# Deformed convolution: GpSimd adds two columns of a neighbourhood to two others in 8 of 20 units, in written order; TensorE turns a unit one unit later

## The chip, the cores and the metric

The kernel runs on one core of a Trainium2 chip. A core has five engines, each with its own queue of instructions that it works off in order: TensorE (PE: matrix products, and with the identity as one operand also transposes; its weight loads are shown apart as PEld), VectorE (DVE), ScalarE (ACT), GpSimd (POOL) and SyncE (SP, which here only issues DMAs). Engines wait for each other through semaphores. Data lies in SBUF (128 partitions), and TensorE writes its results to PSUM, which ScalarE and VectorE read. The metric is the device time of one execution in microseconds (us), as the median of several runs. A profiled execution gives a trace of every instruction.

## The reference, cut to what matters

The whole computation is a small network of four layers on an image of 256 channels and 64 x 64 points. The change concerns layer 1, a deformable convolution (3 x 3 points, 8 groups of 32 channels):

```python
v = x_nhwc @ w_in + b_in
f = gelu(layer_norm(depthwise_conv_3x3(x)))
offset = (f @ w_off + b_off).reshape(B, H, W, G, P, 2)
mask = softmax((f @ w_mask + b_mask).reshape(B, H, W, G, P), axis=-1)
# each of the 9 points of a group is read bilinearly at its shifted place
sampled = gather(y0, x0) * (1 - wx) * (1 - wy) + gather(y0, x1) * wx * (1 - wy) \
        + gather(y1, x0) * (1 - wx) * wy       + gather(y1, x1) * wx * wy
out = (sampled * mask).sum(points) @ w_out + b_out
y = batch_norm(out);  return y * sigmoid(y)
```

The offsets are small (under one point), so the kernel does not gather: each output point is a weighted sum over the 5 x 5 neighbourhood of `v`, with 25 weights for each point and group that it works out from offsets and mask. The input is checked for that at the end, and another path, not run here, is there for larger offsets.

## The kernel before, in words

`layer1_near` runs over 8 blocks (`b`), each of 4 image rows in the upper half and 4 in the lower half: partitions are 64 columns of the upper half and 64 of the lower. A block is worked in 20 **units** `(r, dy)`: row `r` (0 to 3) of the block times row `dy` (0 to 4) of the neighbourhood, in the order r, then dy. In what follows a unit has its number 5r + dy, 0 to 19.

For a unit, one multiplication forms the five products of the neighbourhood's columns `dx` with their weights, as a tile `pr` of 128 x 1280 (5 columns x 256 channels). Then TensorE transposes each of the five columns in two halves of 128 channels, and all these transposes accumulate in one PSUM tile `acc`: the transposes are at once the turn from points to channels and the sum over the 25 neighbours. A unit has 10 transposes of 128 x 128; I call them the unit's **turn** (L1152 to L1156). For dy = 0 to 3 VectorE makes the product (L1150), into one of three buffers (`bufs=3`), with weights that ScalarE has copied to PSUM (`l_w_ps`, L1132, one buffer for two rows r). For dy = 4 GpSimd makes it (L1145, `pr4`, one buffer), and it is issued when the row's unit dy = 0 is written.

After units 9 and 19 ScalarE copies `acc` (L1160), two output projections follow (`project`, L1163 to L1169: TensorE, then Silu on ScalarE, then an add on VectorE), and at the end of a block the results are turned back to tokens (`tokens`, L1171). These go through a list, `late`, from which one entry is taken after each unit.

Beside the units of block b, work for later blocks is woven in, by the number of the unit at which it is written:

- `near_offsets(b + 2)`: the depthwise convolution as 18 taps, two each at units 0 to 8 (ScalarE scales a shifted image, L1011 and L1013, into one of three buffers, and TensorE turns and accumulates it with 4 transposes, L1015); the layer norm at unit 9 on VectorE (statistics L1022, scaling `l_n` L1029); turns and Gelu at 15 and 16 (L1036, L1038); the projection to offsets and mask at 18 and 19 (L1043, one PSUM buffer, read by VectorE in L1044). Blocks 0 to 5 have this.
- `near_weights(b + 1)`: from these offsets and masks the 25 weights, mostly on GpSimd: the softmax's subtraction (`powers`, unit 0, L1068) and division (`shares`, unit 2, L1083), `across` (unit 4, L1086), `columns` 0, 1 and 2 (units 6, 8 and 10, L1094 and L1097: 3, 4 and 4 instructions), `rows` (units 11 to 15, L1105 to L1109). VectorE and ScalarE give it maxima, sums, exponentials and hat functions. Blocks 0 to 6 have this.

Within `manual_schedule` (L953) TensorE's instructions keep the order in which they are written. The order on the other engines is decided by a scheduler. On GpSimd it has put all of a block's `near_weights` between the `pr4` of row 0 and that of row 1.

Of the kernel before, what the change touches and what calls it, by code (L numbers as in the profile page):

```python
# [10 lines left out]
F32 = mybir.dt.float32  # L11
# [3 lines left out]
ALU = mybir.AluOpType  # L15
# [4 lines left out]
P = 128  # L20
# [60 lines left out]
def bc(ap, axis, n):  # L81

    ap = ap.unsqueeze(axis)
    shape = list(ap.shape)
    shape[axis] = n
    return ap.to_broadcast(shape)


class Net:
# [28 lines left out]
    def weights(self, pool, names):  # L118

        for i, name in enumerate(names):  # L120
            src = self.A[name].rearrange("(k p) n -> p k n", p=P)
            w = pool.tile(list(src.shape), F32, tag=name, name=name)
            eng = self.nc.sync if i % 2 == 0 else self.nc.scalar
            eng.dma_start(out=w, in_=src)
            self.w[name] = w
# [785 lines left out]
    def layer1_near(self, y, t, xd, pool, dpool, wp, ps):  # L911
        nc, w = self.nc, self.w
        bn_s, bn_t = self.bn(pool)


        vt = dpool.tile([VW, VW, C], F32, tag="vt", name="vt")
        zero = pool.tile([P, 2 * C], F32, tag="zero", name="zero")
        nc.gpsimd.memset(zero, 0.0)
        for at in (0, VW - 2):
            edge = vt[at : at + 2].rearrange("a b c -> (a b c)").rearrange("(p k) -> p k", p=P)  # L920
            nc.scalar.dma_start(out=edge, in_=zero[:, : edge.shape[1]])
            nc.scalar.dma_start(out=vt[2 : HW + 2, at : at + 2, :].rearrange("a b c -> a (b c)"), in_=zero[:HW, :])
        def values(b):
            vs = wp.tile([P, TPB, C], F32, tag="vs", name="l1_v", bufs=2)
            for i in range(0, TPB, 2):
                p = ps.tile([P, 2, C], F32, tag="acc", name="l1_v_ps", bufs=2)
                for j in range(2):
                    r = b * TPB + i + j
                    for kt in range(2):
                        for h in range(2):  # L930
                            nc.tensor.matmul(p[h * HW : (h + 1) * HW, j, :], y[:, kt, h, r + 1, 1 : HW + 1],
                                             w["w_in1"][:, kt, :], start=(kt == 0), stop=(kt == 1))
                nc.vector.tensor_add(vs[:, i : i + 2, :], p, bc(self.row("b_in"), 1, 2))
            for h in range(2):
                r0 = HH * h + b * TPB + 2
                nc.sync.dma_start(out=vt[2 : HW + 2, r0 : r0 + TPB, :], in_=vs[h * HW : (h + 1) * HW])

        vks = []
        def chunk(k):

            vk = pool.tile([P, 5, 2, C], F32, tag="vk", name="l1_vk", bufs=4)
            for h in range(2):
                for dx in range(5):
                    r0 = HH * h + 2 * k
                    nc.sync.dma_start(out=vk[h * HW : (h + 1) * HW, dx], in_=vt[dx : dx + HW, r0 : r0 + 2, :])
            vks.append(vk)

        spare = pool.tile([P, NBLK], F32, tag="spare", name="l1_spare")


        offsets = lambda b: self.near_offsets(b, y, wp, ps)
        weights = lambda b, om: self.near_weights(b, om, spare, wp)
        with self.tc.manual_schedule(engines={mybir.EngineType.PE}):  # L953
            om, wg = {}, {}
            om[0], todo = offsets(0)
            for b in range(NBLK):
                values(b)
                for _, go in todo[3 * b : 3 * b + 3]:
                    go()
            for k in range(3):  # L960
                chunk(k)
            for _, go in todo[3 * NBLK :]:
                go()
            wg[0], todo = weights(0, om[0])
            om[1], more = offsets(1)
            for _, go in todo + more:
                go()
            late = []
            for b in range(NBLK):
                beside = []  # L970
                if b + 1 < NBLK:
                    wg[b + 1], todo = weights(b + 1, om[b + 1])
                    beside += todo
                if b + 2 < NBLK:
                    om[b + 2], todo = offsets(b + 2)
                    beside += todo
                units, end = self.near_products(b, xd, t, wg[b], vks, chunk, bn_s, bn_t, wp, ps)
                for u, unit in enumerate(units):
                    late += unit()
                    for at, go in beside:  # L980
                        if at == u:
                            go()
                    if late:
                        (late.pop(0) or (lambda: 0))()
                late += end
            for go in late:
                go and go()

        low = pool.tile([P, 1], F32, tag="low", name="l1_low")
        nc.vector.tensor_reduce(low, spare, AX.X, ALU.min)  # L990
        nc.vector.tensor_single_scalar(self.flags[:, 0:1], low, 0.0, ALU.is_lt)
# [123 lines left out]
    def near_products(self, b, xd, t, wg, vks, chunk, bn_s, bn_t, wp, ps):  # L1115
# [3 lines left out]
        nc, w = self.nc, self.w  # L1119
        R = TPB  # L1120
# [3 lines left out]
        def start(i):  # L1124
            if i == 0:
                for m in range(2):
                    nc.scalar.dma_start(out=sx[:, m], in_=xd[m].rearrange("p (h r x) -> p h r x", h=2, x=HW)[:, :, b * R : (b + 1) * R])
                    nc.scalar.activation(sx[:, m], sx[:, m], AF.Identity, bias=self.par("bout0", m))
            if 2 * b + i + 3 < 2 * NBLK + 2:
                chunk(2 * b + i + 3)  # L1130
            held["w"] = ps.tile([P, 2, 5, 5, NH], F32, tag="w", name="l1_w_ps")
            nc.scalar.copy(held["w"].rearrange("p r a b g -> p (r a b g)"), wg[:, 2 * i : 2 * i + 2].rearrange("p r a b g -> p (r a b g)"))  # L1132
            held["acc"] = ps.tile([P, 2, 2, P], F32, tag="acc", name="l1_acc_ps", bufs=2)

        def unit(r, dy):
            i, j = r // 2, r % 2
            if j == 0 and dy == 0:
                start(i)
            acc, at = held["acc"], r + dy
            vk = vks[2 * b + at // 2][:, :, at % 2, :].rearrange("p d (g c) -> p d g c", c=D)  # L1140
            if dy == 0:

                vk4 = vks[2 * b + (r + 4) // 2][:, :, r % 2, :].rearrange("p d (g c) -> p d g c", c=D)
                held["pr4"] = wp.tile([P, 5, NH, D], F32, tag="pr4", name="l1_pr4", bufs=1)
                nc.gpsimd.tensor_tensor(held["pr4"], vk4, bc(wg[:, r, 4], 3, D), ALU.mult)  # L1145
            if dy == 4:
                pr = held["pr4"]
            else:
                pr = wp.tile([P, 5, NH, D], F32, tag="pr", name="l1_pr", bufs=3)
                nc.vector.tensor_tensor(pr, vk, bc(held["w"][:, j, dy], 3, D), ALU.mult)  # L1150
            pf = pr.rearrange("p d g c -> p d (g c)")
            for dx in range(5):  # L1152
                for m in range(2):
                    nc.tensor.matmul(acc[:, m, j, :], pf[:, dx, m * P : (m + 1) * P], self.ident, is_transpose=True,  # L1154
                                     start=(j == 0 and dy == 0 and dx == 0 and m == 0),
                                     stop=(j == 1 and dy == 4 and dx == 4 and m == 1))  # L1156
            if j == 0 or dy < 4:
                return []
            aT = wp.tile([P, 2, 2 * P], F32, tag="aT", name="l1_aT")
            nc.scalar.copy(aT, acc.rearrange("p m j q -> p m (j q)"))  # L1160
            return [None] + [(lambda m: lambda: project(i, aT, m))(m) for m in range(2)]

        def project(i, aT, m):  # L1163
            o = ps.tile([P, 2, 2, HW], F32, tag="o", name="l1_o_ps")
            self.mm(o.rearrange("p j h x -> p (j h x)"), [(w["w_out1"][:, kt, m * P : (m + 1) * P], aT[:, kt, :]) for kt in range(2)])
            sl = wp.tile([P, 2, 2, HW], F32, tag="sl", name="sl")
            nc.scalar.activation(sl, o, AF.Silu, bias=bn_t[:, m : m + 1], scale=bn_s[:, m : m + 1])
            xs = sx[:, m, :, 2 * i : 2 * i + 2].rearrange("p h r x -> p r h x")
            nc.vector.tensor_add(xs, xs, sl)  # L1169
# [1744 lines left out]
```

## Time and profile before

| what | value |
|---|---|
| median of 3 runs | 3446.09 us (3445.12 to 3449.45) |
| profiled execution, its own time | 3443.01 us |
| its span in the profile | 3441.5 us |
| TensorE busy in the span | 3103.2 us (90%) |
| VectorE busy | 2311.1 us (67%) |
| GpSimd busy | 1457.5 us (42%) |
| stretch of layer 1's units | 1097 to 1433 us of the span |
| transposes of units (L1154) in it | 1600 |

The page gives busy times over the whole span, and most of the span is other layers. What matters here are the 336 us from 1097 to 1433 us, in which the eight blocks are worked; so the stretch's own tables are read: busy time by engine, what an instruction waited for, and the timeline. Two things help in reading them. A merged row of the timeline gives when a group started and how long it lasted, with the modelled end of the last matrix product in it. And idle time of an engine is printed with what ended it.

### The profile page before, as it was taken

The page shows a single profiled execution, that of the slowest core. Times are in us where ns is not written, and L with a number is a line of the kernel's source. Part 1 is how long each engine was busy: PE and PEld are TensorE (multiplying, and loading weights), DVE is VectorE, ACT ScalarE, POOL GpSimd, SP SyncE. Part 2 cuts the span into 40 slices and gives each one's busy share as a digit, 9 for nine tenths or more (in the row PEclk, how much of TensorE's full clock was granted, in tenths as well). Part 3 has the DMA queues.
Part 4 walks back from the last instruction along what each step waited for, and adds up shares of the span by engine and source line. Part 5 has one row for each costly group of instructions (what it writes and reads, how often), then busy time and mean ns, then how long its engine had stood idle before and what let it go on. Part 6 is the DMA issues. An engine that isn't in the chain of part 4 may idle for free.

```text
span 3441.5 us, 66218 instructions
## 1 busy us (share of the span) xinstructions
PE 3103.2 (90%) x25772; PEld 2319.7 (67%) x25772; DVE 2311.1 (67%) x5339; ACT 1327.2 (39%) x2554; POOL 1457.5 (42%) x1323
## 2 busy tenths in 40 slices
PE   6779999999977899896969789999999996999997
PEld 3443444344436888665857567888888885999996
DVE  8885777577754677796855576777777775555552
ACT  4444334444425666242633352222222222333331
POOL 2028788778843555326344352000000003555552
PEclk9889999999988999897979899999999997999998
DMA  2146556521134222100158643323333214555554
GB/s 74 40 114 142 161 154 168 130 68 52 48 116 111 68 74 73 44 1 2 52 183 264 215 181 127 98 86 98 99 99 98 91 64 154 200 194 199 206 206 176
DMA packets 241688, 407.01 MB, mean 118 GB/s; under 512 B 78353, under 2 KB 152850, under 8 KB 231890
## 3 DMA queue, kind: packets, MB, share of 16 engines
q1 hardware_dynamic: 212002, 344.40, 32.2%
q0 software_dynamic: 13056, 35.93, 2.8%
q10 hardware_dynamic: 16304, 22.31, 1.9%
q8 instruction: 207, 3.39, 0.4%
q14 instruction: 119, 0.97, 0.1%
HBM read 287.07 MB, written 111.30 MB: 116 GB/s over the span
## 4 chain that ended last, share of the span: by engine, by line
PE 42%; DVE 9%; DMA 5%; issue 5%; ACT 3%; POOL 3%; SPq 0%; POOLq 0%; DVEq 0%; ACTq 0%
PE a_sa_ps L2537 6%; PE f_h_ps L146 5%; DMA ys<-f_y,f_at 3%; PE l_acc_ps L1154 3%; PE a_oa_ps L2576 3%; PE a_ob_ps L2576 3%; PE a_oc_ps L2576 3%; PE a_sb_ps L2537 3%; PE f_ya_ps L146 2%; PE f_yb_ps L146 2%; POOL ys L2292 2%; DVE l_pr L1150 2%; PE a_od_ps L2576 1%; PE a_q_ps L146 1%; PE a_qkv_ps L146 1%
## 5 line engine op out<-in xcount | busy, mean ns | idle before, releaser
L770 ACT COPY l_sc<-l_s 128x384 f32<-128x384 f32 (+1 forms) x632 | 304.0, 532 | 456.9 <-PE l_s L763 445.0
L775 DVE TENSOR_TENSOR l_sm<-l_s,mask 128x256 f32<-128x256 f32 (+2 forms) x628 | 308.2, 552 | 89.2 <-PE l_s L763 88.0
L2103 POOL DMA_INDIRECT xs<-f_room,f_to x64 | 64.5, 1007 | 698.0 <-issue 582.4
L146 PE MATMUL f_h_ps<-f_xT,f_w 128*128 128x256 f32 x1440 | 341.1, 388 | 19.4 <-DVE f_xT L2212 9.7
L146 PEld LDWEIGHTS f_h_ps<-f_xT,f_w 128*128 128x128 f32 x1440 | 262.2, 192 | 84.0 <-ACT f_h L2222 31.3
L763 PE MATMUL l_s<-l_q,l_k 32*128 32x256 f32 (+3 forms) x2944 | 270.5, 453 | 0.0
L2556 ACT ACTIVATE a_e<-a_e 128x512 f32<-128x512 f32 x256 | 156.0, 629 | 246.2 <-DVE a_e L2526 245.2
L780 POOL TENSOR_TENSOR l_sm<-l_sc,mask 128x768 f32<-128x768 f32 (+1 forms) x116 | 201.9, 1748 | 88.2 <-ACT l_sc L770 88.1
L2222 ACT ACTIVATE f_h<-f_h_ps,f_w 128x256 f32<-128x256 f32 x360 | 166.6, 470 | 187.9 <-PE f_h_ps L146 178.7
L1150 DVE TENSOR_TENSOR l_pr<-l_vk,l_w_ps 128x1280 f32<-128x1280 f32 x128 | 186.7, 1482 | 55.2 <-PE l_acc_ps L1154 37.6
L763 PEld LDWEIGHTS l_s<-l_q,l_k 32*128 32x128 f32 x2944 | 132.4, 183 | 115.2 <-issue 67.5
L2292 POOL DMA_INDIRECT ys<-f_y,f_at x144 | 145.7, 1012 | 140.6 <-ACT f_y L2291 110.0
L1154 PE MATMUL l_acc_ps<-ident,l_pr 128*128 128x128 f32 x1600 | 198.1, 278 | 7.7 <-POOL l_pr L1145 7.6
L1154 PEld LDWEIGHTS l_acc_ps<-ident,l_pr 128*128 128x128 f32 x1600 | 184.7, 144 | 14.1 <-POOL l_pr L1145 8.3
L784 POOL TENSOR_TENSOR l_sm<-l_sc,mask 128x256 f32<-128x256 f32 (+1 forms) x220 | 184.9, 868 | 16.1 <-ACT l_sc L770 15.2
L2249 POOL TENSOR_TENSOR f_wt<-f_w 128x512 f32<-128x512 f32 x72 | 89.8, 1268 | 217.1 <-PE f_ya_ps L146 204.9
L2537 PE MATMUL a_sa_ps<-a_q,a_kt 128*128 128x256 f32 x512 | 155.6, 386 | 15.1 <-DVE a_u L2542 14.3
L2541 ACT COPY a_u<-a_sa_ps 128x256 f32<-128x256 f32 x128 | 47.6, 372 | 292.0 <-PE a_sa_ps L2537 292.0
L809 PE MATMUL l_b_ps<-l_sm,l_v 128*32 128x256 f32 (+2 forms) x2176 | 153.7, 372 | 0.0
L2537 PE MATMUL a_sa_ps<-a_qt,a_kt 128*128 128x256 f32 x512 | 152.3, 379 | 0.0
L780 POOL TENSOR_TENSOR l_sm<-l_sc,mask_c 128x768 f32<-128x768 f32 (+1 forms) x64 | 122.9, 1937 | 39.7 <-ACT l_sc L770 39.2
L2537 PE MATMUL a_sb_ps<-a_qt,a_kt 128*128 128x256 f32 x512 | 131.4, 379 | 0.0
(558 smaller groups left out, 7292.1 us busy)
## 6 DMA issues: line engine op xcount, KB each, us to landing
a_kt<-a_kd SPq DMA_DIRECT2D x128, 512.0 KB
f_w<-in_f_w SPq DMA_DIRECT2D x36, 1152.0 KB
f_w<-in_f_w SPq DMA_DIRECT2D x36, 1028.0 KB
xs<-zero SPq DMA_DIRECT2D x8, 4160.0 KB
l_vk<-vt SPq DMA_DIRECT2D x180, 128.0 KB
f_x<-xs SPq DMA_DIRECT2D x72, 260.0 KB
f_w<-in_f_w SPq DMA_DIRECT2D x36, 384.0 KB
l_rcp<-l_recd SPq DMA_DIRECT2D x48, 256.0 KB
```

Source lines behind the costliest of these rows:

```text
L146: self.nc.tensor.matmul(out, lhsT, rhs, start=(i == 0), stop=(i == len(pairs) - 1))
L763: nc.tensor.matmul(s[pair, j][:, at : at + m, :], key(hp), qs[hp], start=(z == 0), stop=(z == len(pieces) - 1))
L770: nc.scalar.copy(sc[:, j], s[1, j])
L775: nc.vector.tensor_tensor(to(pair, j, kind, at), pick(s[pair, j], kind, which), mask, ALU.mult)
L780: nc.gpsimd.tensor_tensor(out[:, :, at, :], of[:, :, which, :], bc(mask, 1, 2), ALU.mult)
L784: nc.gpsimd.tensor_tensor(to(1, j, kind, at), pick(sc[:, j], kind, which), mask, ALU.mult)
L1150: nc.vector.tensor_tensor(pr, vk, bc(held["w"][:, j, dy], 3, D), ALU.mult)
L1154: nc.tensor.matmul(acc[:, m, j, :], pf[:, dx, m * P : (m + 1) * P], self.ident, is_transpose=True, start=(j == 0 and dy == 0 and dx == 0 a ...
L2222: nc.scalar.activation(h[:, m, :], q, AF.Gelu, bias=w1[:, 2 * hidden + m : 2 * hidden + m + 1])
L2292: nc.gpsimd.indirect_dma_start(out=self.ys_parts[(i % 4) * NI + k], in_=y[:, k, :], in_offset=None, out_offset=bass.IndirectOffsetOnAxis(a ...
L2537: mm = lambda out, i, right: nc.tensor.matmul(out, A[i], right, start=True, stop=True)
L2576: nc.tensor.matmul(out, vs[:, j, i, :], right, start=(j == 0 and side != 1), stop=(j == NPAIR - 1 and side != 0))
```

## The change

Four things change in the units.

1. In units with dy = 1 or 3 (8 of 20) GpSimd adds columns 2 and 3 of the product tile to columns 0 and 1, in place (an add of 128 x 512), and TensorE then turns only the columns 0, 1 and 4: 6 transposes instead of 10.
2. The turn of a unit is written one unit later: `unit()` now returns a function, and the loop calls it in the next unit (`behind`), before that unit's woven work. `after` keeps a block's end in place behind it.
3. GpSimd's instructions, too, keep the order in which they are written.
4. In the block's last row (r = 3) VectorE makes the product of dy = 4 too, so GpSimd has three `pr4` in a block and not four.

```diff
-        with self.tc.manual_schedule(engines={mybir.EngineType.PE}):
+        with self.tc.manual_schedule(engines={mybir.EngineType.PE, mybir.EngineType.Pool}):
...
-            late = []
+            late, behind, after = [], lambda: [], []
...
                 for u, unit in enumerate(units):
-                    late += unit()
+                    use = unit()
+                    late += behind() + after
+                    behind, after = use, []
                     for at, go in beside:
                         if at == u:
                             go()
                     if late:
                         (late.pop(0) or (lambda: 0))()
-                late += end
-            for go in late:
+                after = end
+            for go in late + behind() + after:
...
-            if dy == 0:
+            by_pool = r < R - 1
+            if dy == 0 and by_pool:
...
-            if dy == 4:
+            if dy == 4 and by_pool:
                 pr = held["pr4"]
...
-            for dx in range(5):
-                for m in range(2):
-                    nc.tensor.matmul(acc[:, m, j, :], pf[:, dx, m * P : (m + 1) * P], self.ident, is_transpose=True,
+            columns = range(5)
+            if dy in (1, 3):
+                nc.gpsimd.tensor_tensor(pf[:, 0:2], pf[:, 0:2], pf[:, 2:4], ALU.add)
+                columns = (0, 1, 4)
+
+            def use():
+                for dx in columns:
+                    for m in range(2):
+                        nc.tensor.matmul(acc[:, m, j, :], pf[:, dx, m * P : (m + 1) * P], self.ident, is_transpose=True,
...
+            return use
```

More of the change, by code (lines that the diff above doesn't have):

```diff
@@ L1151, in unit @@
             pf = pr.rearrange("p d g c -> p d (g c)")
-            for dx in range(5):
-                for m in range(2):
[L1154 to L1161, printed above, removed]
+            columns = range(5)
[6 more added lines that the diff above has]
+                        nc.tensor.matmul(acc[:, m, j, :], pf[:, dx, m * P : (m + 1) * P], self.ident, is_transpose=True,
+                                         start=(j == 0 and dy == 0 and dx == 0 and m == 0),
+                                         stop=(j == 1 and dy == 4 and dx == 4 and m == 1))
+                if j == 0 or dy < 4:
+                    return []
+                aT = wp.tile([P, 2, 2 * P], F32, tag="aT", name="l1_aT")
+                nc.scalar.copy(aT, acc.rearrange("p m j q -> p m (j q)"))
+                return [None] + [(lambda m: lambda: project(i, aT, m))(m) for m in range(2)]
+            return use
         def project(i, aT, m):
```

## The prediction

> **What bounds the kernel now.** I read the stretch of layer 1's units alone, 1097 to 1433 us. First its busy times, by parts: a steady block, then block 6 up to its unit 11, then the rest (columns: length, busy time of PE, PEld, DVE, ACT, POOL, granted clock, DMA share, GB/s).
>
> ```profile
> core 0: us, PE busy (x) PEld busy (x) DVE busy (x) ACT busy (x) POOL busy (x), PEclk, DMA share, GB/s
> 1231.70:1276.05 44.35, 40.41 (x323) 38.52 (x322) 32.09 (x40) 29.88 (x45) 25.36 (x24) 0.96 0.25 72
> 1364.60:1390.50 25.90, 19.71 (x142) 18.43 (x141) 18.61 (x19) 10.91 (x16) 20.37 (x22) 0.87 0.25 72
> 1390.50:1433.00 42.50, 39.42 (x325) 37.15 (x323) 31.74 (x29) 8.73 (x16) 12.22 (x8) 1.00 0.16 41
> ```
>
> A steady block takes 44.3 us, TensorE is busy 91% of it; VectorE has 12 us to spare, GpSimd 19. Second, who waits for whom in the stretch:
>
> ```profile
> POOL l_pr L1145 <- PE l_acc_ps L1154: 83.3, 16, 6.5
> DVE l_pr L1150 <- PE l_acc_ps L1154: 37.6, 33, 5.2
> PE l_f_ps L1015 <- ACT l_tap L1013: 13.7, 6, 2.5
> PE l_acc_ps L1154 <- POOL l_pr L1145: 7.6, 2, 4.0
> ```
>
> VectorE and GpSimd wait for TensorE to free their buffers; TensorE waits little for products. So it is the bound, with gaps. Third, prices, by form (mean ns of one after the busy time; the last row is from later, the nearest to the new add: in place, 128x512, two inputs):
>
> ```profile
> L1154 PE MATMUL l_acc_ps<-ident,l_pr 128*128 128x128 f32 x1600 | 198.1, 278 | 7.7 <-POOL l_pr L1145 7.6
> L1150 DVE TENSOR_TENSOR l_pr<-l_vk,l_w_ps 128x1280 f32<-128x1280 f32 x125 | 182.3, 1482 | 51.6 <-PE l_acc_ps L1154 37.6 <-ACT l_w_ps L1132 12.6 <-DMA l_vk<-vt 0.2
> L1094 POOL TENSOR_TENSOR l_tx<-l_ax,l_hat 128x288 f32<-128x288 f32 x35 | 28.5, 829 | 0.6
> L1094 POOL TENSOR_TENSOR l_tmp<-l_ax,l_hat 128x288 f32<-128x288 f32 x28 | 21.9, 804 | 0.0
> L1097 POOL TENSOR_TENSOR l_tx<-l_tx,l_tmp 128x576 f32<-128x576 f32 x14 | 19.9, 1418 | 0.6
> L1145 POOL TENSOR_TENSOR l_pr<-l_vk,l_wg 128x1280 f32<-128x1280 f32 x31 | 72.8, 2348 | 95.4 <-PE l_acc_ps L1154 83.3 <-issue 9.0 <-DMA l_vk<-vt 3.1
> L1674 POOL TENSOR_TENSOR t<-t,pr 128x512 f32<-128x512 f32 x16 | 17.5, 1093 | 0.0
> ```
>
> Last, the timeline of a steady block, at the points that I measure from, and one row of block 6:
>
> ```profile
> 1231.57 1.25 PE L1154 MATMUL l_acc_ps<-ident,l_pr 128*128 128x128 f32 x10
> 1245.50 1.25 PE L1154 MATMUL l_acc_ps<-ident,l_pr 128*128 128x128 f32 x10
> 1253.87 2.35 POOL L1145 TENSOR_TENSOR l_pr<-l_vk,l_wg 128x1280 f32<-128x1280 f32 x1
> 1259.46 1.25 PE L1154 MATMUL l_acc_ps<-ident,l_pr 128*128 128x128 f32 x10
> 1260.75 1.49 DVE L1150 TENSOR_TENSOR l_pr<-l_vk,l_w_ps 128x1280 f32<-128x1280 f32 x1
> 1275.88 1.26 PE L1154 MATMUL l_acc_ps<-ident,l_pr 128*128 128x128 f32 x10
> ...
> 1383.73 4.53 PE L1154 MATMUL l_acc_ps<-ident,l_pr 128*128 128x128 f32 x20 [3.54 <-POOL l_pr L1145]
> ```
>
> These are the turns of unit 0 (T0, right after the second offset projection), 4, 11 and the next T0; 1253.87 is row 1's pr4, 1260.75 unit 15's product. Ten turns back to back advance by 1.09 us (pitch 0.109; the modelled end hangs over by 0.16). So a block has three parts: **I**, T0 to the end of turn 4, 15.03; **II**, to the end of turn 11 (1260.55), 13.95; **III**, to the next T0, 15.33. The row at 1383.73 shows what a wait costs afterwards: 20 transposes in 4.53 us, 0.227 each, at a granted clock of 0.50 (1383.7 to 1388.2).
>
> **The change part by part.**
>
> *Fewer transposes:* 8 x 4 in a block, 32 x 0.109 = 3.5 us of TensorE, 28 us in all; a gain where TensorE stays the bound.
>
> *Adds in written order.* The build order of the changed kernel on GpSimd is, after T0: softmax subtraction, add 1, division, add 3, `across`, pr4 of row 1, add 6, `columns` 0, add 8, `columns` 1, pr4 of row 2, `columns` 2, add 11, `rows` with add 13, adds 16, 18, the next pr4. Row 1's pr4 has one buffer and waits for turn 4. Before, it stood behind all weights too, but only unit 9 needed it, at 1256.27; it was done at 1256.22. Now turn 11 needs add 11, and between turn 4 and that lies, on one queue: 2.35 (pr4) + 1.09 + 3 x 0.83 + 1.09 + (2 x 0.80 + 0.83 + 1.42) + 2.35 + (the same 3.85) + 1.09 = 18.2 us, and 0.2 for two semaphores. TensorE has only this to do meanwhile: turns 5 to 10 (52 transposes, 5.7), taps of four units (8 groups of 4, 3.5), two token turns (0.9), a projection (1.0): 11.1 us. It waits 7.3 us, mostly before turn 11, then makes that turn at half clock, 6 x 0.227 = 1.4. Part II becomes 19.8: **+5.8**. Queued behind turn 11 on TensorE is the second output projection and every later turn; VectorE's unit 15 waits for the buffer that turn 11 frees.
>
> The add is not in the trace. Low: 1.05 (the scaling in place of L1671). High: 1.47 (L2249's form with `f_wt` as input and output). I take L1674's 1.09, which is an add in place like this one; 1.47 makes II 1.1 longer.
>
> *One unit later, and the last row's product on VectorE.* Part III is VectorE's: in before, from unit 15's product, through scaling `l_n`, three products, the weight copy, three products, to L1044, which frees the PSUM buffer that the second offset projection waits for (1.47 us of wait there). In the built order it is after `l_n` units 16 to 19, the copy and next unit 0: five products in place of six. **-1.4** (one at 1.43 back to back). TensorE's 22 transposes fewer in III (turns 12 to 18, 58, for 12 to 19, 80) are beside it: no further gain. The bound: 0 if add 16 or 18 holds up TensorE's first projection, -2.9 if the copy's wait (0.6) and the clock are better too.
>
> *Part I* has the same TensorE work (turns 19 to 4 are 52 transposes in place of 50) and the same chain of L1044, maximum, subtraction, exponential, tap, which in before stops TensorE for 2.45 us. But ScalarE's built order now puts the Silu of the first output projection behind the fourth to sixth tap and a table load (1.28), and the second projection waits for it. Worked along the queue this is 0.4 to 1.2 later; I take **+0.8**, ends 0 and 2. Adds 1 and 3 are done 1 us before their turns.
>
> *Sum.* A steady period gets +5.8 - 1.4 + 0.8 = +5.2. There are five from T0 to T0 (1142.9 to 1364.5): +26. Block 0: unit 4 a slot later (+1.0), part II 19.8 instead of 18.8 (1108.47 to 1127.28, TensorE waited 4.0 for pr4 there already), -1.4: +0.6. Block 6, without taps: T0 to the end of turn 11 was 25.95; now `across` ends at +9.3, pr4 starts at +9.7, and with 18.4 and 1.4 it is 29.5: +3.5. Block 6's end and block 7, 35.8 us before: TensorE saves 44 x 0.109 = 4.8, but VectorE makes 22 products instead of 20 (22 x 1.44, eight adds of 0.42, three copies' waits of 0.6: 36.9), and twice a pr4 and an add (3.5) stand against 2 us of TensorE work: +2, ends -3 and +4. Total **+32**, on 3443.0: 3475. That execution is 3.1 us under the median of the runs shown, 3446.1; on the median it is **3478**. SP's queue is the same; outside the stretch nothing moves.
>
> *Two rules against the trace.* The Trainium skill, "TensorE: Matmul & The Clock Gate", Part 4, says that the full clock does not engage for transposes. Here 90 transposes from 1391.28 took 9.99 us at a clock of 1.00, so the rule does not hold; by it the 256 transposes saved would be worth 58 us. The same page's closing table wants no idle gap over about 3 us; the trace is stricter: after 2.45 us idle (1236.09 to 1238.54) the clock was 0.59 until 1242.7. By either, a 7 us wait is followed by slow turns.
>
> **The rivals.**
>
> 1. *TensorE stays the bound* (other side). Its work per block falls by 3.5 us, and nothing waits: -28, **3418**. For it: 91% busy, GpSimd idle 19 us a block, and it would be busy 32 of 41. Against it: it needs GpSimd's 18.4 us to be at most about 13 (the point where the period is 44.3 again), and the prices and the buffer's wait leave no room.
> 2. *It comes out even*, within 7 us: the waits of part I (2.45 and 1.1) vanish and III takes its lower end: +5.0 - 2.9 - 2.0 = 0.1 a period; **3448**. Against it: the exponential's chain is untouched.
> 3. *Worse*: adds of 1.47, half clock also in parts I and III: +5.8 + 1.1 + 2 + 0 = +8.9 a period, five of them 45, with block 0 (2), 6 (5) and the end (4) +56: **3502**. For it: GpSimd's add may price like L2249.
> 4. *It does not do what it says*: excluded, since the built order has 64 adds on GpSimd and 1344 turns' transposes.
>
> **How the numbers follow.** Forecast 0.72, worse 0.15, even 0.06, TensorE-bound 0.07. What can be told from no change is 0.2%, 7 us. Low end of the likeliest: 3.4 a period (no slow clock, part I at 0, adds 1.05), +17, and the tail -3: 3460; I reach to 3453 for part of the even case. High: 3502, the worse case. Slower 0.88, same 0.05, faster 0.07.
>
> **What would show it.** Right: a steady period of about 49.5 us; "PE l_acc_ps <- POOL l_pr" near 5 to 7 us a block, in turn 11, with a clock near 0.5 behind it; GpSimd's pr4 of row 2 back to back with the two `columns`; VectorE's unit 15 right after turn 11. Wrong: a period under 44, or TensorE waits spread over VectorE's products. An add far from 1.09 us, or `columns` slowed beside the adds, would miss the size.

## The result, and the profile after

The changed kernel takes 3483.9 us (median of 4 runs, 3478.2 to 3491.0), the kernel before 3447.4 us beside it (3445.1 to 3449.5). The ratio is 1.0107, with a 95% interval of 1.0087 to 1.0127: slower, by 36.5 us, where 32 were forecast. The profiled execution took 3485.17 us (span 3483.4), 42.2 more than the profiled execution of before.

In the trace, the stretch of layer 1's units begins with the second offset projection ahead of them (1096.32 us before, 1094.17 after) and ends with a DMA that loads the next layer's `w_qkv` (1430.00 and 1470.57). That is 333.7 us before and 376.4 after, 42.7 more: the whole loss lies in the stretch. First, the busy times of the changed kernel (columns as in the table of before): a steady block from T0 to T0, block 6 up to the end of its turn 11, and the rest.

```profile
core 0: us, PE busy (x) PEld busy (x) DVE busy (x) ACT busy (x) POOL busy (x), PEclk, DMA share, GB/s
1244.12:1292.90 48.78, 37.97 (x290) 35.45 (x289) 34.91 (x41) 29.99 (x45) 32.70 (x31) 0.93 0.23 66
...
1391.89:1425.10 33.21, 20.16 (x131) 18.07 (x130) 21.54 (x20) 11.27 (x17) 25.57 (x24) 0.85 0.19 56
1425.10:1470.57 45.47, 37.25 (x277) 33.09 (x275) 35.19 (x28) 7.34 (x14) 22.18 (x18) 0.96 0.10 30
```

This block is 4.4 us longer than the one shown of before (the mean over five is 5.0), and no engine is busy more than 78% of it: TensorE has less work and more time. Second, the waits in the stretch, 1097 to 1471 us (who waits for whom: total us, number, longest):

```profile
PEld l_acc_ps L1163 <- POOL l_pr L1157: 70.7, 27, 7.4
PE l_acc_ps L1163 <- POOL l_pr L1157: 62.5, 21, 7.0
DVE l_pr L1153 <- PE l_acc_ps L1163: 61.7, 32, 6.5
POOL l_pr L1157 <- DVE l_pr L1153: 42.7, 18, 4.1
POOL l_pr L1148 <- PE l_acc_ps L1163: 38.6, 9, 6.0
```

Before, TensorE waited 7.6 us for GpSimd in the whole stretch; now it waits 62.5 us, all of it for the new add (L1157). Third, the prices, by form:

```profile
L1153 DVE TENSOR_TENSOR l_pr<-l_vk,l_w_ps 128x1280 f32<-128x1280 f32 x133 | 194.0, 1481 | 79.1 <-PE l_acc_ps L1163 61.7 <-ACT l_w_ps L1134 10.6 <-DMA l_vk<-vt 5.6
L1163 PE MATMUL l_acc_ps<-ident,l_pr 128*128 128x128 f32 x1344 | 179.7, 287 | 62.9 <-POOL l_pr L1157 62.5 <-DVE l_pr L1153 0.2
L1157 POOL TENSOR_TENSOR l_pr<-l_pr 128x512 f32<-128x512 f32 x64 | 82.0, 1282 | 44.3 <-DVE l_pr L1153 42.7 <-DMA l_vk<-vt 1.6
L1148 POOL TENSOR_TENSOR l_pr<-l_vk,l_wg 128x1280 f32<-128x1280 f32 x23 | 54.1, 2352 | 38.6 <-PE l_acc_ps L1163 38.6
```

The add takes 1.28 us, not the 1.09 that I took. VectorE's product kept its price beside the adds (1.48 us before and after), so the loss is not a slower VectorE. Last, the timeline of the steady block: T0, row 1's `pr4`, `columns` 1's last instruction, row 2's `pr4`, add 11, turn 11, unit 15's product, and the next T0. (In the changed kernel the turn at T0 is that of unit 19, written one unit late.)

```profile
1244.12 1.25 PE L1163 MATMUL l_acc_ps<-ident,l_pr 128*128 128x128 f32 x10
...
1259.26 2.35 POOL L1148 TENSOR_TENSOR l_pr<-l_vk,l_wg 128x1280 f32<-128x1280 f32 x1 [5.27 <-PE l_acc_ps L1163]
...
1268.61 1.42 POOL L1099 TENSOR_TENSOR l_tx<-l_tx,l_tmp 128x576 f32<-128x576 f32 x1
...
1269.99 2.34 POOL L1148 TENSOR_TENSOR l_pr<-l_vk,l_wg 128x1280 f32<-128x1280 f32 x1
...
1276.08 1.26 POOL L1157 TENSOR_TENSOR l_pr<-l_pr 128x512 f32<-128x512 f32 x1
...
1277.39 1.54 PE L1163 MATMUL l_acc_ps<-ident,l_pr 128*128 128x128 f32 x6 [7.03 <-POOL l_pr L1157]
...
1279.04 1.49 DVE L1153 TENSOR_TENSOR l_pr<-l_vk,l_w_ps 128x1280 f32<-128x1280 f32 x1 [5.68 <-PE l_acc_ps L1163]
...
1292.90 1.25 PE L1163 MATMUL l_acc_ps<-ident,l_pr 128*128 128x128 f32 x10
```

GpSimd starts row 1's `pr4` when turn 4 has freed its buffer, and from there it is busy without a gap until add 11: 1259.26 to 1277.34. TensorE has nothing left from 1270.36 on and waits 7.03 us. Turn 11 starts when add 11 ends, and runs slowly: its six transposes take 1.34 us to the start of the next projection at 1278.73, 0.22 each. The windows around it show the granted clock (third column from the right):

```profile
1270.30:1277.39 7.09, 0.06 (x1) 0.00 (x1) 3.06 (x4) 3.33 (x4) 7.09 (x7) 0.84 0.00 0
1277.39:1280.40 3.01, 3.01 (x10) 2.58 (x11) 1.36 (x1) 0.00 (x0) 2.93 (x6) 0.50 0.04 8
```

### The profile page after: what moved, and what is told of

It is laid out like the page before. It is cut to its first block, busy times and chain, and to the rows that moved or that the text cites. A ratio compares the mean times of both kernels' runs of the same rounds, so it can differ in the third digit from the quotient of the medians.

```text
span 3483.4 us, 65789 instructions
## 1 busy us (share of the span) xinstructions
PE 3091.9 (89%) x25516; PEld 2301.6 (66%) x25516; DVE 2345.7 (67%) x5347; ACT 1326.5 (38%) x2554; POOL 1517.0 (44%) x1379
## 4 chain that ended last, share of the span: by engine, by line
PE 64%; DVE 14%; DMA 7%; POOL 5%; issue 5%; ACT 4%; SPq 1%; ACTq 0%; POOLq 0%; DVEq 0%
PE l_s L763 9%; PE a_sa_ps L2548 6%; PE f_h_ps L146 5%; PE l_b_ps L809 4%; DMA ys<-f_y,f_at 3%; PE a_oa_ps L2587 3%; PE a_ob_ps L2587 3%; PE a_oc_ps L2587 3%; PE l_a_ps L809 3%; PE a_sb_ps L2548 3%; PE l_x_ps L146 3%; PE f_ya_ps L146 2%; PE l_c_ps L809 2%; PE f_yb_ps L146 2%; PE l_acc_ps L1163 2%
## 5 line engine op out<-in xcount | busy, mean ns | idle before, releaser
L1153 DVE TENSOR_TENSOR l_pr<-l_vk,l_w_ps 128x1280 f32<-128x1280 f32 x136 | 198.4, 1481 | 83.5 <-PE l_acc_ps L1163 61.7
L1163 PE MATMUL l_acc_ps<-ident,l_pr 128*128 128x128 f32 x1344 | 179.7, 287 | 62.9 <-POOL l_pr L1157 62.5
L1163 PEld LDWEIGHTS l_acc_ps<-ident,l_pr 128*128 128x128 f32 x1344 | 162.1, 149 | 75.7 <-POOL l_pr L1157 70.7
L780 POOL TENSOR_TENSOR l_sm<-l_sc,mask_c 128x768 f32<-128x768 f32 (+1 forms) x64 | 121.0, 1906 | 39.3 <-ACT l_sc L770 38.7
```

The lines of the kernel that those rows point to most:

```text
L780: nc.gpsimd.tensor_tensor(out[:, :, at, :], of[:, :, which, :], bc(mask, 1, 2), ALU.mult)
```

## The experiments

**The theory**: the adds make TensorE late, because they stand on a queue in written order behind a `pr4` that waits for its one buffer and behind two `columns`. **Rivals**: the turn one unit later or the moved product of the last row loses the time; or each add costs its share, wherever it stands. No variant leaves out a part of the computation: where adds are taken away, those units make all ten transposes again. The runs were made on several chips, whose times differ by up to 2%, so only the ratio to the kernel before on the same chip is compared. The period is that of five steady blocks, between the starts of the second offset projections; the "end" is from the last of these to the `w_qkv` load. Both come from one profiled execution of each kernel. Expectations in microseconds stand against 3447 us.

| kernel | ratio (95%) | period, us | end, us |
|---|---|---|---|
| before | 1 | 44.3 | 67.1 |
| before, GpSimd in written order | 0.9983 (0.9973 to 0.9992) | 44.3 | 66.9 |
| after | 1.0107 (1.0087 to 1.0127) | 49.3 | 80.2 |
| no adds | 0.9958 (0.9941 to 0.9974) | 43.4 | 63.7 |
| two buffers for `pr4` | 1.0084 (1.0067 to 1.0101) | 47.9 | 75.7 |
| `columns` 2 one unit later | 1.0076 (1.0059 to 1.0093) | 47.8 | 74.0 |
| GpSimd ordered by the scheduler | 1.0113 (1.0096 to 1.0130) | 48.2 | 82.9 |
| adds 1, 3, 13, 16, 18 | 1.0048 (1.0026 to 1.0069) | 47.1 | 73.3 |
| adds 6, 8, 11 | 1.0134 (1.0118 to 1.0151) | 51.2 | 76.7 |
| adds 1, 3, 6, 8, 16, 18 | 0.9999 (0.9988 to 1.0009) | 44.1 | 72.9 |
| adds 1, 3, 16, 18 | 0.9966 (0.9952 to 0.9980) | 42.5 | 69.7 |
| adds 11, 13 | 1.0100 (1.0083 to 1.0116) | 49.4 | 74.5 |
| adds 11, 13; `columns` 2 behind add 13 | 0.9988 (0.9979 to 0.9998) | 44.7 | 69.6 |
| adds 1, 3, 16, 18 in blocks 0 to 5 | 0.9935 (0.9919 to 0.9952) | 42.6 | 65.2 |

### 1. No adds

```diff
-                nc.gpsimd.tensor_tensor(pf[:, 0:2], pf[:, 0:2], pf[:, 2:4], ALU.add)
-                columns = (0, 1, 4)
+                pass
```

> The changed kernel without GpSimd's adds: every unit is turned with 10 transposes again; written order, later turn and VectorE's product in the last row stay. Theory (the queue on GpSimd from pr4 of row 1 to add 11 holds up turn 11): no turn waits for an add, part II falls from 19.7 to the 13.0 to 13.9 us of TensorE's work, parts I and III stay near 15.5 and 14.2; a steady period near 43.2 us, 1.1 under before's 44.3, block 6 loses its 3.5 us wait too: 3432 to 3442 us. Rival (written order, the later turn or VectorE's extra product cost the time): the period stays above 46 us and the time above 3455 us.

Measured: ratio 0.9958, which is 3433 us on 3447; the period is 43.4 us. The other three parts of the change are a gain of 0.4%, and the adds cost 1.5%, net of the transposes that they save. The rival that the later turn or the moved product loses the time falls.

### 2. Two buffers for `pr4`

```diff
-  held["pr4"] = wp.tile([P, 5, NH, D], F32, tag="pr4", name="l1_pr4", bufs=1)
+  held["pr4"] = wp.tile([P, 5, NH, D], F32, tag="vs", name="l1_pr4", bufs=2)
```

(The other tag is one whose space lies free here.)

> The changed kernel with two buffers for GpSimd's products of dy = 4 (they take over the place of an earlier tile, vs, that is no longer needed). Theory: pr4 of row 1 no longer waits for turn 4 and starts some 5 us earlier, but add 8 then waits for VectorE's product of unit 8, whose buffer turn 5 frees, so only about 2 us of the 7 us wait before turn 11 go: a period near 47.2 us, 3474 us. Rival (the one buffer is the cause): the wait before turn 11 goes to under 2 us, a period of 44.5 us, 3455 us.

Measured: 1.0084, period 47.9 us, near what the theory has; the rival's 44.5 us falls. The buffer is worth 1.4 us of the 5.0. The waits between 1100 and 1430 us and the turn 11 of one block in this kernel:

```profile
POOL l_pr L1157 <- DVE l_pr L1153: 50.4, 23, 4.2
PE l_acc_ps L1163 <- POOL l_pr L1157: 45.5, 15, 7.0
```

```profile
1221.24 1.54 PE L1163 MATMUL l_acc_ps<-ident,l_pr 128*128 128x128 f32 x6 [5.42 <-POOL l_pr L1157]
```

TensorE still waits 5.4 us in turn 11. With `pr4` earlier, GpSimd's adds wait for VectorE's products instead (50.4 us in total; between the same times the changed kernel has 31.3, and 55.9 for TensorE's waits): in a written order an add that comes too early blocks `columns`, which could have run.

### 3. `columns` 2 and the rows one unit later

```diff
-  [(6 + 2 * kx, call(columns, kx)) for kx in range(3)]  ...  [(11 + dy, call(rows, dy)) for dy in range(5)]
+  [((6, 8, 11)[kx], call(columns, kx)) for kx in range(3)]  ...  [(12 + dy, call(rows, dy)) for dy in range(5)]
```

> The changed kernel with the third group of columns written at unit 11 instead of 10, behind add 11, and the rows one unit later (12 to 16). Theory: the queue from turn 4 to add 11 is 3.7 us shorter, the wait before turn 11 falls from 7 to about 3.3 us, a wait of up to 1.8 us before turn 13 appears beside VectorE's work; a period near 45.2 us, 3455 to 3463 us. Rival (the adds cost by their number and price, wherever they stand): GpSimd's work is the same, so the time stays within 5 us of the changed kernel's.

Measured: 1.0076, or 3474 us, period 47.8 us: more than the theory's 3455 to 3463, and 10 us below the changed kernel, where the rival allowed 5. The mechanism was half right. Turn 11 waits 3.26 us, but `columns` 2 are now ahead of add 13, and in some blocks turn 13 waits too. The timeline of one such block:

```profile
1219.55 0.88 PE L1163 MATMUL l_acc_ps<-ident,l_pr 128*128 128x128 f32 x6 [3.26 <-POOL l_pr L1157]
...
1224.98 3.61 PE L1163 MATMUL l_acc_ps<-ident,l_pr 128*128 128x128 f32 x16 [2.59 <-POOL l_pr L1157]
```

The second wait, 2.59 us, is followed by turns 13 and 14 in 3.6 us (16 transposes, 0.226 each). So in this block, and in one more of the five, the time came back one turn later. In the other three turn 11 itself ran slowly behind its wait of 2.6 to 3.3 us, and turn 13 waited 1.2 us or not at all. I had looked only at the turn whose wait I moved.

### 4. GpSimd ordered by the scheduler

```diff
-        with self.tc.manual_schedule(engines={mybir.EngineType.PE, mybir.EngineType.Pool}):
+        with self.tc.manual_schedule(engines={mybir.EngineType.PE}):
```

> The changed kernel with GpSimd's order left to the scheduler, which puts add 3 behind all three groups of columns and pr4 of row 1 behind all of the block's weights. Theory: turn 3 waits for add 3 until about T0 + 20 us instead of being due at 13.4, so part I grows by some 7 us to 22, and part II shrinks to 13.5 since add 6 to add 11 then stand close together: a period near 49.7 us, 3475 to 3490 us, with the wait moved from turn 11 to turn 3. Rival (the written order is what costs): a period near 43 us, under 3447 us.

Measured: 1.0113, within the interval of the changed kernel; period 48.2 us. I had expected the wait in turn 3 and a period of 49.7. The scheduler puts all `columns` and `rows` ahead of add 6, not of add 3, so the wait stands in turn 6 instead of turn 11 (GpSimd's last row and add 6, then turn 6, in this kernel):

```profile
1219.58 0.32 POOL L1107 COPY l_wg<-l_tx 128x160 f32<-128x160 f32 x1
1219.85 1.26 POOL L1157 TENSOR_TENSOR l_pr<-l_pr 128x512 f32<-128x512 f32 x1
```

```profile
1221.17 1.34 PE L1163 MATMUL l_acc_ps<-ident,l_pr 128*128 128x128 f32 x6 [3.59 <-POOL l_pr L1157]
```

So it is not the written order as such. And written order does no harm to the kernel before either:

### 5. The kernel before, with GpSimd in written order

```diff
-        with self.tc.manual_schedule(engines={mybir.EngineType.PE}):
+        with self.tc.manual_schedule(engines={mybir.EngineType.PE, mybir.EngineType.Pool}):
```

> The kernel before with one edit: GpSimd's instructions in written order. Theory: row 1's pr4 no longer stands behind all weights, so the waits for it in block 0 (4.0 us) and block 6 (3.5 us) go; the steady period stays near 44.3 us: ratio 0.997 to 0.998, which would be most of what the changed kernel without adds gains (0.9958). Rival (the later turn or VectorE's product in the last row makes that gain): ratio 0.999 to 1.001.

Measured: 0.9983 (0.9973 to 0.9992), a gain of about 0.2%, with the steady period and the end unchanged. The gain is in block 0, where TensorE waited 4 us for a `pr4` before: from its second offset projection to the next one it takes 39.3 us instead of 45.1. The wait for a `pr4` in block 6, which I expected to count as well, is gone without making the end shorter. Together with the first experiment this gives the parts of the change: written order -0.2%, the later turn and the moved product about another -0.2% (period 43.4 instead of 44.3, end 63.7 instead of 66.9), the adds +1.5%.

### 6. and 7. The adds ahead of turn 11: without them, and they alone

The theory of the prediction was that adds 6, 8 and 11 lie on the chain from turn 4 to turn 11, and the others do not.

```diff
-            if dy in (1, 3):
+            if 5 * r + dy in (1, 3, 13, 16, 18):
```

> The changed kernel with five of the eight adds (units 1, 3, 13, 16, 18); units 6, 8 and 11, whose adds stand in the queue between turn 4 and turn 11, are turned with 10 transposes. Theory: the 7 us wait is gone as without any add, and TensorE has 20 transposes fewer; part I 15.3, II 12.9, III 14.2, a period near 42.4 us, ratio to before 0.993 to 0.996. Rival (the adds cost by their number): five eighths of the 1.5% between no adds and all, ratio near 1.005.

```diff
-            if dy in (1, 3):
+            if 5 * r + dy in (6, 8, 11):
```

> The changed kernel with only the adds of units 6, 8 and 11. Theory: these three make the whole loss, so turn 11 still waits some 7 us, part II stays near 19.7, part I is near 16.4 and III near 14.5 as without adds; a period near 50 us, ratio to before 1.009 to 1.014. Rival (by number): three eighths, ratio near 1.002.

Measured: the three adds alone give 1.0134, as expected: they suffice for the whole loss. But without them the ratio is 1.0048, what the rival by number had, and the theory in this form falls. The timeline of the kernel without them shows why:

```profile
1214.60 2.35 POOL L1148 TENSOR_TENSOR l_pr<-l_vk,l_wg 128x1280 f32<-128x1280 f32 x1 [1.53 <-PE l_acc_ps L1163]
...
1219.45 1.39 POOL L1099 TENSOR_TENSOR l_tx<-l_tx,l_tmp 128x576 f32<-128x576 f32 x1
...
1221.65 1.45 POOL L1157 TENSOR_TENSOR l_pr<-l_pr 128x512 f32<-128x512 f32 x1
...
1223.16 3.67 PE L1163 MATMUL l_acc_ps<-ident,l_pr 128*128 128x128 f32 x16 [3.63 <-POOL l_pr L1157]
```

Row 2's `pr4` cannot start before turn 9 has freed the buffer. Behind it come `columns` 2, two `rows`, and only then add 13, for which turn 13 waits 3.63 us, again with slow turns behind. So the theory was changed: what costs is *any* add that stands behind row 2's `pr4` and `columns` 2, and that is the add of unit 11 and the add of unit 13. This makes a sharp test against the rival by number, with two kernels whose adds are each other's complement.

### 8. to 10. The adds behind `columns` 2: left out, and alone

```diff
-            if dy in (1, 3):
+            if 5 * r + dy in (1, 3, 6, 8, 16, 18):
```

> The changed kernel with the adds of units 11 and 13 alone left out (their turns go back to 10 transposes; the same output). The theory as it stands after the adds 6, 8 and 11 were left out: what TensorE waits for is any add that GpSimd runs behind columns 2, because columns 2 stand behind the third pr4 product, which can start only once turn 9 has freed the one pr4 buffer. Only the adds of units 11 and 13 are there. Without them no turn waits more than about 1.5 us (unit 16, whose add stands behind the rows, is the one that may), the period comes to some 44 to 45.5 us and the ratio to the kernel before to 0.994 to 1.002, about 0.998. The rival, that each add costs its share wherever it stands, has six eighths of the 1.5% between no adds and all of them: about 1.007.

```diff
-            if dy in (1, 3):
+            if 5 * r + dy in (1, 3, 16, 18):
```

> The changed kernel with the adds of units 1, 3, 16 and 18 alone (6, 8, 11 and 13 left out; the same output). Theory: adds 6 and 8 end just before their turns need them, so taking them out as well moves the third pr4 product by some 0.4 us at most, since it waits for turn 9; period 43.8 to 45.3 us, ratio 0.994 to 1.001, within 0.003 of the kernel without adds 11 and 13. Rival by number: four eighths of 1.5%, about 1.003.

```diff
-            if dy in (1, 3):
+            if 5 * r + dy in (11, 13):
```

> The changed kernel with the adds of units 11 and 13 alone. Theory: they make nearly the whole loss by themselves: turn 11 waits some 6 us (third pr4 product 2.35 us from turn 9, columns 2 3.8 us, add 1.28 us, less the turn 10 that lies beside them), so the period is 48 to 50.5 us and the ratio 1.007 to 1.014. Rival by number: two eighths of 1.5%, about 0.9995.

Measured: without adds 11 and 13, six adds cost nothing against before (0.9999, where the rival by number had 1.007). Those two alone cost 1.0% (1.0100, where it had 0.9995), with the period of the changed kernel, 49.4 us. The rival by number falls. The queue in the kernel with these two alone:

```profile
1220.31 2.35 POOL L1148 TENSOR_TENSOR l_pr<-l_vk,l_wg 128x1280 f32<-128x1280 f32 x1 [1.52 <-PE l_acc_ps L1163]
1222.62 1.80 POOL L1096 TENSOR_TENSOR l_tmp<-l_ax,l_hat 128x288 f32<-128x288 f32 x2
1224.38 0.79 POOL L1096 TENSOR_TENSOR l_tx<-l_ax,l_hat 128x288 f32<-128x288 f32 x1
1225.13 1.39 POOL L1099 TENSOR_TENSOR l_tx<-l_tx,l_tmp 128x576 f32<-128x576 f32 x1
1226.48 1.26 POOL L1157 TENSOR_TENSOR l_pr<-l_pr 128x512 f32<-128x512 f32 x1
...
1227.79 1.54 PE L1163 MATMUL l_acc_ps<-ident,l_pr 128*128 128x128 f32 x6 [5.60 <-POOL l_pr L1157]
```

From the end of turn 9 to turn 11 there are 7.4 us of GpSimd's work, and TensorE waits 5.6 of them in each of the five blocks. One expectation was missed: taking out adds 6 and 8 as well gave more than I thought (0.9966, 0.0033 below the kernel with them, period 42.5 us, not 43.8 to 45.3). They end in time for their turns, but they push row 2's `pr4` back by 0.9 us (10.72 us from the start of row 1's `pr4` to that of row 2's, against 9.82 without them). How the 1.7 us of the period follow from that is not shown.

### 11. The same two adds, with `columns` 2 behind them

If the place in the queue makes the price, the same two adds must become cheap when they stay and the queue is changed.

```diff
-            if dy in (1, 3):
+            if 5 * r + dy in (11, 13):
...
-  [(6 + 2 * kx, call(columns, kx)) for kx in range(3)]  ...  [(11 + dy, call(rows, dy)) for dy in range(5)]
+  [((6, 8, 13)[kx], call(columns, kx)) for kx in range(3)]  ...  [(14 + dy, call(rows, dy)) for dy in range(5)]
```

> The changed kernel with the adds of units 11 and 13 alone, as in the run before, which gave 1.0100 and a wait of 5.6 us before turn 11 in every block; and now columns 2 written at unit 13, behind the add of unit 13, with the rows at units 14 to 18 (the same output). Theory, that the place in GpSimd's queue makes the price and not the adds themselves: only the third pr4 product (2.35 us from the end of turn 9) is left ahead of add 11, so turn 11 waits about 1.5 to 2.5 us, turn 13 under 1 us, the period falls from 49.3 to 43.5 to 45.5 us and the ratio from 1.010 to 0.996 to 1.003. If the adds of units 11 and 13 cost by themselves, or the columns only move the same wait to another turn (the late rows, then the first product of the next block), the ratio stays at 1.006 to 1.011.

Measured: 0.9988, period 44.7 us; the 1.0% loss is gone. The timeline of this kernel:

```profile
1209.87 2.34 POOL L1148 TENSOR_TENSOR l_pr<-l_vk,l_wg 128x1280 f32<-128x1280 f32 x1 [1.53 <-PE l_acc_ps L1163]
...
1212.17 2.74 POOL L1157 TENSOR_TENSOR l_pr<-l_pr 128x512 f32<-128x512 f32 x2
...
1213.48 0.87 PE L1163 MATMUL l_acc_ps<-ident,l_pr 128*128 128x128 f32 x6 [1.74 <-POOL l_pr L1157]
...
1215.06 3.00 PE L1163 MATMUL l_acc_ps<-ident,l_pr 128*128 128x128 f32 x26
```

Both adds now follow row 2's `pr4` at once. Turn 11 waits 1.74 us, as the theory had, turns 12 to 14 follow without a wait, and they run at full speed.

### 12. The four adds in the blocks with taps alone

In blocks 6 and 7 there are no taps, so TensorE has less other work to do while a turn waits for an add. So adds should be left out of them. In the other blocks the four adds are kept that were a gain in experiment 9.

```diff
-            if dy in (1, 3):
+            if 5 * r + dy in (1, 3, 16, 18) and b < NBLK - 2:
```

> The changed kernel with the adds of units 1, 3, 16 and 18 alone, and these in blocks 0 to 5 only (blocks 6 and 7 turn ten transposes in every unit; the same output). With these four adds in all blocks the ratio was 0.9966: the period was 42.5 us (44.3 before, 43.4 without adds), but from the last offset projection to the end of the stretch it took 69.7 us (67.1 before, 63.7 without adds). Theory: an add pays where TensorE is the bound, in the blocks that carry the taps, and costs where it is not, in blocks 6 and 7. Then the period stays at 42.3 to 42.9 us, the end takes 63 to 66 us, and the ratio is 0.992 to 0.996, below both. Rival: the longer end has another cause than the adds there (the clock, or the queue left over from block 5); then the end stays near 69 us and the ratio at 0.9960 to 0.9975.

Measured: 0.9935 (0.9919 to 0.9952), period 42.6 us, end 65.2 us: as the theory expected, and 0.65% faster than the kernel before. Its interval overlaps that of no adds (0.9941 to 0.9974), so it is not shown to be the fastest of all. Busy times of this kernel, and then of the one with the four adds in all blocks, over the end (columns as before):

```profile
1348.85:1414.08 65.23, 60.03 (x477) 56.86 (x477) 55.19 (x49) 18.60 (x31) 27.95 (x25) 0.97 0.17 50
```

```profile
1344.52:1414.22 69.70, 59.02 (x445) 54.34 (x445) 56.54 (x49) 18.60 (x31) 37.97 (x33) 0.95 0.16 46
```

With 32 instructions more, TensorE is done 4.5 us earlier there. The theory's reason, that TensorE is not the bound there, is not shown: it is still the busiest engine, 60.0 of 65.2 us. The four adds of the blocks with taps are a gain: 42.6 us a period against 43.4 without any add.

One thing in these two traces limits what they can tell. Block 0 has the same instructions in both kernels, and it took 41.9 us here, at a granted clock of 0.91, and 38.3 us in the other, at 1.00. So layer 1's stretch is 320.1 us here and 320.2 there (333.7 before, on another chip): the profiled executions account for 13.6 of the 22.4 us between the medians of this kernel and of before, and where the rest lies is not shown.

## Why the prediction was right

The direction and the mechanism were right, and the steady period within 0.2 us. The terms of the sum were not equally good, and it was luck that they cancel: part I was 0.7 us too long in the forecast, part III 0.6 too short. From T0 to T0, as means over the five steady blocks (end of turn 4 taken as 0.24 us before row 1's `pr4`, end of turn 11 as the start of the projection behind it):

| term | forecast | measured |
|---|---|---|
| part I | +0.8 | +0.1 (15.2 us) |
| part II | +5.8 | +5.7 (19.65 us) |
| part III | -1.4 | -0.8 (14.5 us) |
| steady period | +5.2 | +5.0 (49.3 us) |
| five periods | +26 | +25.0 |
| block 0 | +0.6 | +4.6 (49.7 against 45.1 us) |
| block 6 to turn 11 | +3.5 | +7.3 (33.2 against 25.95 us) |
| from there to the end | +2 | +5.9 (45.5 against 39.6 us) |
| sum | +32 | +42.8 |

*Part II* carried the forecast and held, with a mistake in it that another one hid. The queue from row 1's `pr4` to the end of add 11 was put at 18.2 us; turn 11 started 18.13 us after that `pr4`. But each of the three adds took 1.28 us and not 1.09, 0.56 more together. The `columns` were shorter from start to start (2.29, 3.65 and 3.79 us instead of 2.49, 3.85 and 3.85), since the instructions of a group overlap a little: the sum of their durations counts that overlap twice. The row that I priced the add by adds a broadcast row; the new add reads two full inputs. I had called it the nearest because it is in place. A subtraction of 128 x 512 with two full inputs stood in the trace of before at 1.27 us (L2249, `f_wt<-f_w`) and would have been nearer. That the broadcast is the reason for the 0.19 us was not tested. The 0.2 us for two semaphores had no row beside it: in the steady block shown, `pr4` starts 0.24 us after turn 4 has ended, and turn 11 0.05 us after add 11. The Trainium skill, "GPSIMD Engine Reference", section 3.1, has about 2.6 cycles an element for a two-input add; at the page's 1.2 GHz that makes an estimate of 1.11 us for 512 elements, and the trace's 1.28 is above it.

*The slow turn* behind the wait was right: 0.22 us for a transpose at a granted clock of 0.50, for 0.227 forecast.

*Part III* came between the value and its upper bound. That bound was named: "0 if add 16 or 18 holds up TensorE's first projection". In some blocks turn 16 does wait 1.1 us for add 16, and in others it does not; part III is 14.0 to 15.0 us long. *Part I* kept its length nearly. In the block shown TensorE does wait for the later Silu, 0.73 us, within the 0.4 to 1.2 that I worked out; but its wait for the tap is 1.91 us there instead of 2.45.

*The ends* are where the size was missed: +17.8 us for block 0, block 6 and what follows, where 6.1 were forecast. In block 0 the time went into its part I, up to the end of turn 4: 16.9 us from the second offset projection (1094.17 to 1111.02) instead of 12.15 (1096.32 to 1108.47), +4.7 where +1.0 was forecast. The projection itself took 3.22 us instead of 1.70, and turn 2 took 2.34 instead of 1.25, after waits for add 1 (0.52) and for taps (1.17 and 0.62): a slow clock that the sum had not allowed for there. That clock need not come with the change: the kernel of experiment 9 has the same instructions up to turn 4, and there the projection took 1.70 us and this part 13.46, +1.3. In block 6 the forecast had row 1's `pr4` 9.7 us after T0, bound by `across`, although turn 4, for which it waits, ended 10.0 us after T0 in before already. It started after 13.9 us, because the second output projection waited 2.24 us for its Silu with no taps to fill the time, and turns 2 to 4 then ran at a granted clock of 0.58. In before that wait was 2.58 us, and the three turns behind it ran at full speed (30 transposes in 3.44 us), so this slow clock, too, need not come with the wait. These are lines of the changed kernel:

```profile
1398.73 2.07 PE L146 MATMUL l_o_ps<-l_aT,w_out 128*128 128x256 f32 x4 [2.24 <-ACT sl L1178]
1400.60 5.08 PE L1163 MATMUL l_acc_ps<-ident,l_pr 128*128 128x128 f32 x26
```

Behind turn 11 and in block 7 I counted VectorE's products and TensorE's work apart. But two turns of five there now need a product *and* the add behind it, one after the other: seven turns waited 6.6 us for adds between 1425 and 1471 us. Experiments 9 and 12 show that the adds of the last two blocks are a loss of their own: 4.5 us at the end even for four of the eight. By the profiled executions the forecast is 10 us short. By the medians it is 4.5 short, since the profiled execution of before (3443.0) lies 4.4 under the median of its runs, and that of the changed kernel 1.3 above.

*The rivals.* That TensorE stays the bound (3418 us) failed on the chain named against it: it needed GpSimd's queue within 13 us and that took 18.1. Even (3448) needed 2.0 us off part I and 2.9 off part III; they gave +0.1 and -0.8. Its sum also starts from +5.0 for part II, a figure that its working does not give; with the forecast's +5.8 it comes to +0.9 a period. Worse (3502) had the add at 1.47; it was 1.28, though the ends came out longer than the 11 us that it allowed for them. The low end, 3460, leaves out the forecast's own terms for block 0 and block 6, 4.1 us.

*What I had seen too narrowly* is which adds matter. The prediction put the loss on the queue between turn 4 and turn 11, with adds 6, 8 and 11 in it. That is the chain of the changed kernel, but not what must be removed to be rid of it: with these three gone, add 13 takes the place of add 11 (experiment 6). The cause that the runs support is the order on the queue: row 2's `pr4`, then `columns` 2, ahead of an add that a turn needs one or two slots later. What releases this `pr4` differs: turn 9 in the kernels of experiments 6 and 10, where it waits 1.5 us for that turn, and in the changed kernel the queue from row 1's `pr4` on, behind which it starts without a gap.

## What to carry to other kernels

Before giving an idle engine a small piece of a busy engine's work, list what stands ahead of each piece on the idle engine's queue, and what the first of these waits for: 19 us of idle time in a block did not help, since add 11 stood behind work whose first piece, a `pr4`, had to wait for its one buffer (a second buffer took away only 1.4 of the 5.0 us a period). The same two adds cost 1.0% or nothing, depending only on whether `columns` 2, and the rows after them, were written ahead of them or behind. When one wait on such a queue is removed, look at the next consumer of the same queue before counting the gain, and try the moved work block by block: here four adds were a gain in the blocks with taps and a loss in the two without.

## What the runs showed of the hardware

The clock behind a wait does not follow the length of that wait alone. In the kernel with `columns` 2 one unit later, turn 11 came after 3.26 us of idle TensorE and was granted the full clock, and turns 13 and 14, a few microseconds later, came after only 2.59 us and got 0.53 (waits and turns in turn; the clock is the third column from the right):

```profile
1216.29:1219.55 3.26, 0.01 (x1) 0.00 (x0) 3.26 (x3) 3.04 (x4) 3.26 (x3) 1.00 0.00 0
1219.55:1222.39 2.84, 2.83 (x20) 2.44 (x20) 1.81 (x3) 1.33 (x3) 2.84 (x4) 1.00 0.00 0
1222.39:1224.98 2.59, 0.00 (x1) 0.00 (x1) 2.55 (x4) 0.81 (x1) 2.53 (x4) 1.00 0.47 123
1224.98:1228.59 3.61, 3.61 (x18) 3.61 (x19) 2.68 (x4) 0.00 (x0) 3.46 (x6) 0.53 0.72 209
```

In the next block of the same kernel turn 11 came after the same wait of 3.26 us, and its six transposes took 1.33 us to the next projection (1266.86 to 1268.19 us), at a clock of 0.50.

A shorter wait can be paid as well: in the changed kernel TensorE waits 1.91 us for a tap in each steady block, and the turn 1 behind it took 1.48 us in one block (from 1152.35 us, at a clock of 0.59) and 0.82 in the next (from 1201.60, at 1.00). A wait of 1.74 us was followed by full speed (experiment 11), waits of 3.6, 5.6 and 7.0 us by about half (0.50 to 0.52). So in these runs a wait of 1.9 to 3.3 us may or may not be paid a second time. The Trainium skill, "TensorE: Matmul & The Clock Gate", Part 1, says that activity is judged in windows of about 3.4 us that run freely, so that the moment of the change depends on where in a window the work begins. That fits the two outcomes of a 3.26 us wait better than the 3 us limit of its closing table, by which both would be paid. It does not by itself account for the waits of 1.91 and 2.59 us that were paid, which are shorter than a window. The windows themselves can't be seen in these traces.
